# Summing layer 1's first 64 edge columns inside layer 0's last block of a two-layer graph kernel

## The chip, the cores and the metric

The kernel runs on one core of a Trainium2 chip. The metric is the time on the device in microseconds (us) from the start to the end of one launch. The engines have short names here: PE is TensorE's matmul (PEld its weight loads), DVE is VectorE, ACT is ScalarE, POOL is GpSimd, SP is SyncE. Each engine works through its own instructions in the order in which the program issued them, and waits on semaphores where it needs what another engine or a transfer made.

## What is computed

There are 6250 nodes with 256 features each and 100000 edges, sorted by destination, each with a source, a destination and a weight. The reference, cut to what matters:

```python
x = x + gnn0(layernorm(x), src, dst, edge_weight)  # layer 0: node sums over edges, and x @ weight_r
x = x + ffn0(layernorm(x))                         # 8 experts, all used, 256->256->256->256, gated by a softmax
x = x + gnn1(layernorm(x), src, dst, edge_weight)  # layer 1: segment_sum(w * h[src], dst), h = layernorm(x) @ weight
x = x + ffn1(layernorm(x))                         # 32 experts, one per node by argmax, 256->64->256, relu
```

In layer 0 the edges run the other way: row `src` gets the features of `dst`. In layer 1 row `dst` gets those of `src`. Any node may be the source of any edge, so the sum for the first destinations of layer 1 can need the layer-0 result of every node, the last ones too.

## The kernel before, in words

Nodes lie in 49 tiles of 128 (the last has 106). `X` (line 81) keeps all of them in SBUF. `h0` and `h1` (lines 82, 83) are the normalised features of both layers in DRAM, from which edges gather.

**Sort, lines 113 to 538.** The edges come sorted by destination. The first part of the kernel sorts them into tiles of sources for layer 0: `Z` and `ZJ` hold, for each tile of 128 sources, the edges' destinations and weights by group of 4096 edges. It also computes `h0` and the first part of `X`.

**Summing edges.** A column is 128 edges. `weighted` (line 211) gathers their 128 rows of 256 floats with one indirect DMA issued on POOL (line 187), splits the weighted rows into two parts `m` on ACT (line 215) and DVE (line 216); `one_hots` (line 204) makes 0/1 matrices for three columns at once on DVE (line 207); one matmul per column adds it into PSUM `acc` (lines 610 and 777). Layer 0 has 18 columns for each tile, 882 in all. Layer 1 takes the edges as they come, 782 columns (`NREAL`), 8 of which (`CS`) cover on average half a tile; each is matched to a window of half a tile, and neighbouring windows are added (`summed`, lines 752 to 766). `by_weight` (line 191) then turns a tile's sum, multiplies it by the layer's weight and adds it to `X`.

**Dense part.** Layer 0 works in 15 blocks of `1, 1, 2, 3, 4 x 10, 2` tiles (line 287): `begin0` normalises and computes the gates, then for each of 8 experts `hidden0` runs twice (L654, L657) and `outs0` adds the gated product to `X` (L666, L668). `end0` (line 671) normalises a finished block, adds the bias and stores its rows of `h1` (line 680, on SP's queue). Layer 1 works in 16 blocks of `1, 1, 2, 3, 4 x 9, 3, 2, 1` tiles (line 289): `begin1` (line 787) normalises, picks each node's expert and makes the masks, then 16 chunks of two experts each run `hidden1` (L822, L825, L827) and the output matmul (L861); line 868 and the stores after it end a block.

**What sets the order.** The program is written in the order of the PE. `Stream.upto` (line 298) advances the column generator, one column a step, and `aheads` (line 303) plans how many columns are to be issued before each half expert or half chunk, so that the columns of block b+1 are all summed within block b: in the first `parts - rest` places those of the next block, in the last `rest` (4 of 16 in layer 0, 8 of 32 in layer 1) a share of those of the block after. A layer's first block waits for all its columns (lines 687, 837). Gathers run ahead of their use by the buffers of `g`: 12 in layer 0 (line 609), 24 in layer 1 (line 776).

**Between the layers.** After the last `outs0`, line 708 calls `end0` for the last block; its store must land before any gather of layer 1. Then `aggregate_any` (line 711) loads a flag into registers and branches around a loop for badly distributed edges, which isn't run with these inputs. Only then does layer 1 load its weights (lines 716 to 737, 4 MB on ACT's queue) and issue its first gather.

Of the kernel before, what the change touches and what calls it, by code (L numbers as in the profile page):

```python
# [39 lines left out]
LAG = 10  # L40
FAR = -2.0 ** 127
SRC_PAD = 8191
LN_EPS = 1e-5
# [4 lines left out]
def gnn_ffn_kernel(ctx: ExitStack, tc: tile.TileContext, a, out):  # L48

# [35 lines left out]
    def across(name):  # L85

        row = a[name]
        t = const.tile([P, row.shape[0]], F32, name=name + "_b")
        nc.scalar.dma_start(t, bass.AP(tensor=row.tensor, offset=row.offset, ap=[[0, P], [1, row.shape[0]]]))
        return t  # L90
# [15 lines left out]
    good = const.tile([P, 1], F32, name="good")  # L106
    off = const.tile([P, 1], F32, name="off")
    edges_rec, edges_val = a["edges_rec"], a["edges_val"]
# [3 lines left out]
    kept = sorted_ctx.enter_context(tc.tile_pool(name="kept", bufs=1))  # L112
# [63 lines left out]
    bias0 = across("L0_gnn_bias_l")  # L176
    bias0r = across("L0_gnn_bias_r")
# [13 lines left out]
    def by_weight(psum, sums, sT, t, tags):  # L191

        tr = psum.tile([P, 2, P], F32, tag=tags[0], name="tr", bufs=1)
# [4 lines left out]
        ph = psum.tile([P, D], F32, tag=tags[1], name="ph", bufs=tags[2])  # L198
# [5 lines left out]
    def one_hots(pool, dl, j, hots):  # L204

        s = pool.tile([P, SJ, P], F32R, tag="s", name="s", bufs=hots)
        nc.vector.tensor_tensor(s, col[:, None, :].to_broadcast([P, SJ, P]),  # L207
                                dl[:, j:j + SJ, None].to_broadcast([P, SJ, P]), OP.is_equal)
# [10 lines left out]
    def aggregate_any(h, by_dst):  # L219
# [3 lines left out]
        with tc.tile_pool(name="any", bufs=1) as pool, \  # L223
                tc.tile_pool(name="anyp", bufs=1, space=bass.MemoryType.PSUM) as psum:
            with tc.If(flag > 0):
                with tc.For_i(0, ROWS, P) as r:
# [7 lines left out]
                    for t in range(NT):  # L234
# [14 lines left out]
                        for _ in by_weight(psum, sums, sT, t, ("tr", "mm", 2)):  # L249
                            pass  # L250

# [35 lines left out]
    ramp = [1, 1, 2, 3] + [NB] * 10 + [2]  # L287
    blocks0 = [list(range(sum(ramp[:b]), sum(ramp[:b + 1]))) for b in range(len(ramp))]
    ramp = [1, 1, 2, 3] + [NB] * 9 + [3, 2, 1]
# [13 lines left out]
    def aheads(cum, parts, rest):  # L303
# [4 lines left out]
        for b in range(len(cum) - 2):  # L308
# [16 lines left out]
    def check_edges():  # L325
# [26 lines left out]
        nc.vector.tensor_copy(badis[1], bads[1])  # L352
        nc.vector.tensor_scalar(off, bads[1], float(DST_PAD), None, op0=OP.mult)
        nc.vector.tensor_scalar(dl_c, dl_c, off, None, op0=OP.add)
# [182 lines left out]
    nc.vector.tensor_scalar(good, bads[0], 1.0, None, op0=OP.is_lt)  # L537
    sort_ctx.close()
# [4 lines left out]
    with tc.tile_pool(name="layer0", bufs=1) as wp, \  # L543
# [57 lines left out]
        def aggregate0():  # L601
# [13 lines left out]
            while True:  # L615
                yield
# [305 lines left out]
```

## Time and profile before

| what | us |
|---|---|
| median of 3 runs without a profile (2944.88 to 2947.58) | 2945.19 |
| the profiled execution | 3303.56 |
| its span, first to last instruction | 3301.8 |
| sort, until the first gather of layer 0 | 0 to 399.5 |
| layer 0, until its last expert's matmuls | 399.5 to 1946.9 |
| layer 1: first gather at 1956.4, first matmul of an expert's mask at 2046.8 | 1946.9 to 3301.8 |

The profiled execution is 358 us longer than the median without a profile. Its mean granted TensorE clock is 0.926. The engines were busy for these shares of the span: PE 85%, PEld 55%, DVE 60%, ACT 49%, POOL 58%. POOL's busy time is nearly all gathers: 882 in layer 0 (902.8 us) and 782 in layer 1 (773.8 us).

How to read the views: the page cuts the span into 40 slices of 82.5 us, each a digit, the busy share in tenths. The windows view gives the same for any stretch in us, with the number of instructions. The view of waits says which engine and line waited for which, total, times and longest in us. The timeline lists instructions by start and duration, merged where they repeat; what stands in square brackets is how long the engine was idle just before, and what ended it. The chain is the work that ended last, followed back from the end; "another core or an unknown queue" is a wait whose end the profile can't put down to an instruction.

### The profile page before, as it was taken

What the parts mean: (1) busy time and instruction counts of PE and PEld (TensorE: products, weight loads), DVE (VectorE), ACT (ScalarE), POOL (GpSimd) and SP (SyncE); (2) the same over time, 40 slices, a digit from 0 to 9 for tenths busy, and PEclk for the clock granted to TensorE, in tenths of its full rate; (3) what the DMA queues carried; (4) which work ended last, traced back from release to release, by engine and by line L of the source; (5) the groups of instructions that cost most, each with busy time, mean ns of one, the idle gap of its engine ahead of it and who ended that gap; (6) DMA issues with size and microseconds to landing.
All of it is one profiled execution on the core that took longest, in us unless ns stands there. A gap on an engine that the chain in (4) does not pass through costs nothing.

```text
span 3301.8 us, 37412 instructions
## 1 busy us (share of the span) xinstructions
PE 2794.1 (85%) x10471; PEld 1817.4 (55%) x10524; DVE 1993.7 (60%) x4839; ACT 1626.1 (49%) x3842; POOL 1904.3 (58%) x1931
## 2 busy tenths in 40 slices
PE   5888667689999999999999964677898888988899
PEld 3444346555555555555555553555665555656577
DVE  8999856577766765655655433555555555545451
ACT  6778445445555554554554433444444444444442
POOL 4566565676666666566665126666666556656520
PEclk8999877899999999999999986788999999989999
DMA  4000232233323323233332033332333223323210
GB/s 132 20 20 20 81 107 77 80 90 86 90 82 91 88 79 89 85 87 85 88 91 72 26 91 89 89 92 83 92 94 92 86 82 92 93 86 90 86 47 10
DMA packets 123155, 260.73 MB, mean 79 GB/s; under 512 B 32252, under 2 KB 68920, under 8 KB 122936
## 3 DMA queue, kind: packets, MB, share of 16 engines
q0 software_dynamic: 79872, 218.21, 23.2%
q1 hardware_dynamic: 26984, 28.08, 2.5%
q10 hardware_dynamic: 16080, 11.94, 1.3%
q8 instruction: 86, 1.41, 0.2%
q14 instruction: 133, 1.09, 0.1%
HBM read 238.87 MB, written 19.25 MB: 78 GB/s over the span
## 4 chain that ended last, share of the span: by engine, by line
PE 61%; issue 5%; another core or an unknown queue 4%; DVE 3%; ACT 2%; POOL 1%; DMA 0%; ACTq 0%; DVEq 0%; POOLq 0%
PE ph L654 16%; PE py L861 10%; PE ph L822 9%; PE py L666 9%; PE acc L777 6%; PE acc L610 5%; PE ph L200 1%; ACT m L215 1%; DVE m L216 1%; PE ph L825 1%; PE tr L269 1%; PE pl L795 1%; POOL g L187 1%; PE py L644 1%
## 5 line engine op out<-in xcount | busy, mean ns | idle before, releaser
L187 POOL DMA_INDIRECT g<-h,idx x882 | 902.8, 1024 | 547.3 <-DVE m L216 286.6
L187 POOL DMA_INDIRECT g<-h,src_c x782 | 773.8, 990 | 442.3 <-DVE m L216 187.5
L215 ACT ACTIVATE m<-g,of_z 128x256 fp32r<-128x256 f32 x882 | 391.7, 499 | 336.0 <-PE acc L610 135.9
L215 ACT ACTIVATE m<-g,val_c 128x256 fp32r<-128x256 f32 x782 | 371.1, 502 | 374.7 <-PE acc L777 172.0
L657 ACT ACTIVATE hT<-ph,shift,scale 128x512 f32<-128x512 f32 (+3 forms) x480 | 331.0, 697 | 417.1 <-PE ph L654 246.9
L216 DVE SCALAR_TENSOR_TENSOR m<-g,val_c,m 128x256 fp32r<-128x256 f32 x782 | 360.8, 481 | 242.7 <-ACT m L215 133.0
L861 PE MATMUL py<-w,hm 128*128 128x256 f32 x1568 | 415.4, 400 | 35.0 <-issue 17.5
L666 PE MATMUL py<-wo,hT 128*128 128x256 f32 x1568 | 390.3, 390 | 61.1 <-issue 30.6
L216 DVE SCALAR_TENSOR_TENSOR m<-g,of_z,m 128x256 fp32r<-128x256 f32 x882 | 398.0, 477 | 56.6 <-ACT m L215 40.2
L654 PE MATMUL ph<-nT,w 128*128 128x512 f32 (+3 forms) x960 | 385.9, 537 | 44.5 <-ACT hT L657 37.6
L777 PE MATMUL acc<-m,s 128*128 128x512 f32 x782 | 367.9, 534 | 52.6 <-DVE m L216 39.6
L822 PE MATMUL ph<-nT,w 128*128 128x512 f32 (+3 forms) x1024 | 396.8, 509 | 3.5 <-issue 3.1
L610 PE MATMUL acc<-m,s 128*128 128x512 f32 x882 | 356.1, 506 | 46.2 <-DVE scale L567 26.1
L654 PE MATMUL ph<-hT,w 128*128 128x512 f32 (+3 forms) x960 | 375.1, 525 | 23.6 <-issue 17.4
L666 PEld LDWEIGHTS py<-wo,hT 128*128 128x128 f32 x1568 | 292.1, 193 | 141.7 <-issue 46.3
L861 PEld LDWEIGHTS py<-w,hm 128*128 128x128 f32 x1568 | 301.0, 201 | 92.1 <-issue 21.9
L827 ACT ACTIVATE hm<-ph,b 128x512 f32<-128x512 f32 (+3 forms) x256 | 149.1, 584 | 290.8 <-PE ph L825 115.1
L207 DVE TENSOR_TENSOR s<-col,dl 128x384 fp32r<-128x384 f32 x294 | 162.4, 554 | 210.3 <-PE acc L610 142.8
L654 PEld LDWEIGHTS ph<-nT,w 128*128 128x128 f32 x960 | 179.4, 200 | 199.3 <-issue 139.6
L668 DVE SCALAR_TENSOR_TENSOR X<-py,gate,X 128x256 f32<-128x256 f32 x392 | 187.9, 481 | 164.9 <-PE py L666 78.8
L207 DVE TENSOR_TENSOR s<-col,dl_c 128x384 fp32r<-128x384 f32 x261 | 144.2, 553 | 231.6 <-PE acc L777 135.6
L654 PEld LDWEIGHTS ph<-hT,w 128*128 128x128 f32 x960 | 178.7, 196 | 144.9 <-issue 118.7
(206 smaller groups left out, 3267.1 us busy)
## 6 DMA issues: line engine op xcount, KB each, us to landing
g<-h,idx POOLq DMA_INDIRECT x882
g<-h,src_c POOLq DMA_INDIRECT x782
h<-hs SPq DMA_DIRECT2D x26, 256.0 KB
X<-in_x_dram SPq DMA_DIRECT2D x12, 512.0 KB
w<-in_L_ffn_W_dram ACTq DMA_DIRECT2D x3, 2048.0 KB
h<-hs SPq DMA_DIRECT2D x10, 512.0 KB
out_dram<-o SPq DMA_DIRECT2D x9, 512.0 KB
wo<-in_L_ffn_Wo_dram ACTq DMA_DIRECT2D x1, 2048.0 KB
```

The costliest lines, as they stand in the source:

```text
L187: nc.gpsimd.indirect_dma_start(out=g, out_offset=None, in_=h, in_offset=bass.IndirectOffsetOnAxis(ap=idx, axis=0))
L207: nc.vector.tensor_tensor(s, col[:, None, :].to_broadcast([P, SJ, P]), dl[:, j:j + SJ, None].to_broadcast([P, SJ, P]), OP.is_equal)
L215: nc.scalar.activation(m[:, 0, :], g, AF.Copy, scale=w)
L216: nc.vector.scalar_tensor_tensor(m[:, 1, :], g, w, m[:, 0, :], op0=OP.mult, op1=OP.subtract)
L610: nc.tensor.matmul(acc, s[:, j % SJ, :], m, start=(j == 0), stop=(j == EW - 1))
L654: nc.tensor.matmul(ph[:, :nw], (w1, w2)[layer][:, e, k, m * P:(m + 1) * P], src[:, k, :nw], start=(k == 0), stop=(k == 1))
L657: nc.scalar.activation(hT[:, m, :nw], ph[:, :nw], AF.Relu, bias=shift[:, layer, c:c + 1], scale=scale[:, layer, c:c + 1])
L666: nc.tensor.matmul(py, hT[:, k, j * P:(j + 1) * P], wo[:, e, k, :], start=(k == 0), stop=(k == 1))
L668: nc.vector.scalar_tensor_tensor(X[:, t, :], py, gate[:, j, e:e + 1], X[:, t, :], op0=OP.mult, op1=OP.add)
L777: nc.tensor.matmul(acc, s[:, j % SJ, :], m, start=(i == 0 or j == 0), stop=done)
L822: nc.tensor.matmul(ph[:, :nw], w1f[:, k, c * P:(c + 1) * P], nT[:, k, :nw], start=(k == 0), stop=False)
L861: nc.tensor.matmul(py[:, j, :], now[:, cols], w2[:, c, :], start=False, stop=(c == NC1 - 1), skip_group_check=True)
```

## The change

The change does the following.

- `columns1` takes the place of `aggregate1`. It sums a range of columns. The first range, columns 0 to 63 (`NE = EARLY * GC`), is appended to layer 0's own column stream and planned into layer 0's last block, from its third half expert on. It gathers from `h1[:LIM]`, the rows of all blocks but the last; an edge whose source lies in the last block gets weight 0 and a harmless index. Its sums stay in `first_sums` (5 tiles). The second range, columns 64 to 781, runs in layer 1.
- `missing` builds, from the sorted `Z` and `ZJ` of layer 0, for each of the last block's 3 tiles a matrix (128 sources x 576 destinations) of the weights of those edges of the first 64 columns that were left out, in four matmuls per pair of pieces; it does so in the last block's experts 5, 6 and 7, in the space of `wo`'s first experts. `add_missing` multiplies them by the last block's normalised rows and adds the product to `first_sums`.
- Layer 0's blocks become `1, 1, 2, 3, 4 x 9, 3, 3`, layer 1's `3, 4 x 11, 2`. The store of the block before the last moves from expert 1 to expert 0 of the last block.
- The sums of layer 1's first block (3 tiles) come from `first_sums`, so `by_weight` of these tiles runs right after `end0` of the last block, before any further gather is used.
- Layer 1's weights take the memory of layer 0's `w1` and `w2`. They are loaded in halves from SP's queue at experts 4 and 7 of the last block. The small ones are loaded three blocks before the end. `sel` is made on DVE behind the first `begin1`.
- `aggregate_any` for layer 1 moves to the very end, with a rerun of all of layer 1's dense part (`again`) that the flag skips with these inputs. PSUM and SBUF pools are shared across the layers, and with `reuse_waits="tile"` a tile that reuses memory waits for that memory's users alone.
- `edges0` works on two tiles at a time instead of four.

```diff
-    ramp = [1, 1, 2, 3] + [NB] * 10 + [2]
+    ramp = [1, 1, 2, 3] + [NB] * 9 + [3, 3]
     blocks0 = [list(range(sum(ramp[:b]), sum(ramp[:b + 1]))) for b in range(len(ramp))]
-    ramp = [1, 1, 2, 3] + [NB] * 9 + [3, 2, 1]
+    ramp = [3] + [NB] * 11 + [2]
...
+    def columns1(pool, psum, js, h, idx, w, bufs):
+        hots, ahead, parts, few = bufs
+        first = js.start == 0
+        ends = []
+        def summed(q, acc):
+            yield
+            if first and (q % 2 or q == 2 * NB):
+                s = first_sums[:, q // 2, :]
+            else:
+                s = pool.tile([P, D], F32, tag="sums", name="sums", bufs=few)
+            nc.scalar.activation(s, acc[:, 0, :], AF.Copy)
+            nc.vector.tensor_add(s, s, acc[:, 1, :])
...
+        for j in range(js.start, js.stop + (0 if first else LAG)):
+            if j < js.stop:
...
+                if (j - js.start) % SJ == 0:
+                    s = one_hots(pool, dl_c, j, hots)
+                m = weighted(pool, h, idx[:, j:j + 1], w[:, j:j + 1], ahead, parts)
+                nc.tensor.matmul(acc, s[:, (j - js.start) % SJ, :], m, start=opens, stop=done)
...
@@ aggregate0
+            for _ in columns1(wp, psum, range(NE), h1[:LIM, :], idx_e, w_e, (3, 12, 6, 2)):
+                yield
@@ end0
-                nc.vector.tensor_add(X[:, t, :], X[:, t, :], bias1)
             nc.sync.dma_start(h1[tiles[0] * P:(tiles[0] + n) * P, :].rearrange("(t p) d -> p t d", p=P),
                               hs[:, :n, :])
+            for t in tiles:
+                nc.vector.tensor_add(X[:, t, :], X[:, t, :], bias1)
+            return hs
+        def load1(k, half):
+            if k == 0:
+                x = a["L1_ffn_W1"][:, half * P:(half + 1) * P, :].rearrange("e p h -> p e h")
+                nc.sync.dma_start(w1f[:, half, :].rearrange("p (e h) -> p e h", h=H1), x)
+            else:
+                cs = slice(half * NC1 // 2, (half + 1) * NC1 // 2)
+                x = a["L1_ffn_W2"].rearrange("e h d -> (e h) d").rearrange("(c p) d -> p c d", p=P)
+                nc.sync.dma_start(w2f[:, cs, :], x[:, cs, :])
+        def missing():
+            nc.gpsimd.iota(near, pattern=[[1, NEAR]], base=0, channel_multiplier=0,
+                           allow_small_or_imprecise_dtypes=True)
...
+            for i in range(n_late):
+                pms = [psum.tile([P, 4 * P], F32, tag="mm", name="pm", bufs=3),
+                       psum.tile([P, wide], F32, tag="tr", name="pm_tr", bufs=1)]
+                for c in range(EARLY):
+                    to = wp.tile([P, NEAR], F32R, tag="there", name="to_m", bufs=1)
+                    nc.vector.tensor_scalar(to, near, dst[:, i, c:c + 1], None, op0=OP.is_equal)
...
+                    for u in range(2):
...
+                        nc.tensor.matmul(pms[0], of[:, u, :], to[:, :4 * P], **flags)
+                        nc.tensor.matmul(pms[1], of[:, u, :], to[:, 4 * P:], **flags)
+                nc.scalar.activation(mats[i][:, :4 * P], pms[0], AF.Copy)
+                nc.scalar.activation(mats[i][:, 4 * P:], pms[1], AF.Copy)
+                yield
+        def add_missing(hs, fs):
+            corr = psum.tile([P, 2, D], F32, tag="mm", name="corr", bufs=3)
+            for u, f in enumerate(fs):
+                rows = min(P, NEAR - f * P)
+                for i in range(n_late):
+                    nc.tensor.matmul(corr[:rows, u, :], mats[i][:, f * P:f * P + rows], hs[:, i, :],
+                                     start=(i == 0), stop=(i == n_late - 1))
+                nc.vector.tensor_add(first_sums[:rows, f, :], first_sums[:rows, f, :], corr[:rows, u, :])
...
+        head = 2
+        plans[-1] = [cum[-1] + NE * max(0, u + 1 - head) / (2 * NX0 - 1 - head) for u in range(2 * NX0 - 1)]
+        plans[-1] += [cum[-1] + NE + 1]
...
             for e in range(NX0):
-                if e == 1 and b > 0:
+                if e == (0 if final else 1) and b > 0:
                     end0(blocks0[b - 1])
+                if b == nblk - 3 and e == 3:
+                    small1()
+                    early_columns()
+                if final and e == 5:
+                    fill = missing()
+                if final and e >= 5:
+                    next(fill)
                 sums.upto(plans[b][2 * e])
                 second = hidden0(1, block, e, first)
...
+                if final and e in (NX0 // 2, NX0 - 1):
+                    load1(0, e // (NX0 // 2 + 1))
+                    load1(1, e // (NX0 // 2 + 1))
                 sums.upto(plans[b][2 * e + 1])
                 outs0(block, e, second)
...
-        end0(blocks0[-1])
+        hs = end0(late)
+        add_missing(hs, (0, 1))
+        add_missing(hs, (2,))
+        firsts = []
+        for t in blocks1[0]:
+            sT = wp.tile([P, 2, P], F32, tag="hT0", name="sT", bufs=2)
+            firsts.append(by_weight(psum, first_sums[:, t, :], sT, t, ("agg", 2) if t else ("tr", 1)))
+            next(firsts[-1])
+        for part in firsts:
+            next(part)
+        add_missing(hs, (3, 4))
-    aggregate_any(h1, by_dst=True)
...
+            sums = Stream(columns1(flow, psum, range(NE, NREAL), h1, src_c, val_c, (5, EW + 6, 12, 4)))
+            cum = [0] + [min(CS * (2 * tiles[-1] + 2) + CS // 2, NREAL) + LAG - NE for tiles in blocks1[1:]]
+            plans = aheads(cum, 2 * NC1, [4] + [8] * (len(blocks1) - 1))
+            block = begin1(flow, blocks1[0])
...
+                    if c == NC1 - (3 if b == 0 else 5) and not last:
+                        after = begin1(flow, blocks1[b + 1])
+                end1(flow, tiles, py)
...
+            aggregate_any(psum, h1, True, again)
```

## The prediction

> **What bounds the kernel now.** I first read the page's slices, to see where no engine is full.
>
> ```profile
> span 3301.8 us, 37412 instructions
> PE   5888667689999999999999964677898888988899
> POOL 4566565676666666566665126666666556656520
> PEclk8999877899999999999999986788999999989999
> ```
>
> There are two holes. POOL falls to 1 and 2 around slice 23, in the middle of the span: no gathers in the last part of layer 0. PE falls to 4 and 6 just after that: layer 1 has begun and its matmuls have nothing to work on. The windows view cuts the passage at what happens in it; columns are the stretch, its length, busy us (instructions) of the five engines, granted clock, DMA share and GB/s.
>
> ```profile
> 1850.00:1947.00 97.00, 96.89 (x382) 69.86 (x380) 30.91 (x82) 39.31 (x66) 0.00 (x0) 1.00 0.02 6
> 1947.00:1957.00 10.00, 0.00 (x0) 0.10 (x1) 5.21 (x17) 0.36 (x2) 2.79 (x3) 0.75 0.16 45
> 1957.00:1985.00 28.00, 11.39 (x18) 5.16 (x18) 14.34 (x36) 10.21 (x23) 21.60 (x22) 0.50 0.91 246
> 1985.00:2047.00 62.00, 19.33 (x51) 11.94 (x51) 16.70 (x48) 17.37 (x40) 41.14 (x42) 0.56 0.30 88
> 2047.00:2322.00 275.00, 207.49 (x859) 158.88 (x860) 144.14 (x369) 118.94 (x288) 180.07 (x181) 0.84 0.30 89
> 2322.00:2822.00 500.00, 432.38 (x1622) 291.86 (x1649) 263.57 (x646) 219.72 (x494) 314.08 (x320) 0.94 0.30 89
> 3197.00:3302.00 105.00, 99.25 (x494) 78.52 (x493) 21.00 (x60) 31.68 (x74) 0.00 (x0) 0.99 0.04 13
> ```
>
> Layer 0 ends with 97 us of full PE and an idle POOL. From 1947 to 2047 PE does 31 us of work, at half clock, while POOL gathers. From 2047 to 2322, the one-, two- and three-tile blocks of layer 1, PE is at 75%, POOL at 181 gathers in 275 us. Only then come the steady blocks of 4 tiles, and the last 105 us are PE alone. The timeline shows the seam.
>
> ```profile
> 1949.72 0.36 SPq L680 DMA_DIRECT2D h<-hs  x1
> 1954.05 2.04 POOL L740 IOTA sel<- 128x2048 bf16 x1 [112.07 <-DMA h<-hs]
> 1956.38 1.28 POOL L187 DMA_INDIRECT g<-h,src_c  x1 [0.17 <-issue]
> 1963.45 0.95 POOL L187 DMA_INDIRECT g<-h,src_c  x1 [0.30 <-issue]
> 1969.24 2.50 PE L777 MATMUL acc<-m,s 128*128 128x512 f32 x5 [22.36 <-DVE m L216]
> 2321.72 0.61 PE L855 MATMUL py<-nought 128*128 128x512 bf16 x2
> ```
>
> POOL waited 112 us for the last store of `h1`. An unhindered gather takes 0.95 + 0.30 = 1.25 us. The last row opens the block of tiles 7 to 10; the next ones open 100.3 us apart on average (five blocks to 2823.2). So 374.8 us lie between layer 0's last matmul (1946.9) and tile 7. Last, the waits, and the chain's row for one of them:
>
> ```profile
> ACT m L215 <- remote: 28.1, 12, 17.9
> POOL g L187 <- DVE m L216: 23.1, 28, 3.6
> 2025.58 17.88 another core or an unknown queue x2
> ```
>
> In those 375 us POOL is hardly held back (23.1 us); it is the pace: tile 7 needs 180 columns plus a lag of 10 and 16 ahead, 206 x 1.25 = 258 us after 1956.4, that is 2214 at best. But 50.5 us of the chain there are waits on an unknown queue, one of them 17.9 us, and in the five steady blocks 63.3, 12.7 each. The profiled execution is 3303.6 us against a median of 2945.2; I take these waits as what is likeliest to be missing from a plain run, and sum both with and without them.
>
> **The change part by part.**
>
> *Final block of layer 0.* Two tiles take 5.18 us an expert (L666 groups at 1910.40 and 1915.58), so three take 7.77, 62.2 in all. It now has 64 columns as well. On PE a column costs 0.21 us (two weight loads of L777 take 0.41 at full clock), 13.7 us; `missing` adds 24 short matmuls, about 4. On ACT 64 x 0.50 = 32 beside 21 for L657; on DVE 64 x (0.48 + 0.18) = 42, plus 12 for the gated adds (24 x 0.48), 10 for `missing` (six of about 0.65, by L207's 0.55 for 384 columns, twelve of 0.25, sixteen of 0.2) and 6 for `end0`. All fit below 100 us; POOL is what counts: `end0`, with its table load, took 8.5 us from its first statistics (1905.1) to the issue and a store 3.8 to land, so about 11 us with three tiles; then 64 x 1.25 = 80, then 6 for landing, scaling, matmul and the last `outs0`. The iota of `missing` stands in POOL's queue and waits for `outs0` of expert 4, which waits for the columns before it: everything gathered after it loses the lead, about 7. Sum 104: layer 0 ends 42 us later than it would (its total dense work is the same with 3, 3 as with 4, 2). Bounds: 35 with no hold by the iota, 59 at the 275/181 = 1.52 us a gather of the small blocks.
>
> *The 4 MB of weights.* They leave the seam and join these gathers. The trace: from 1957 to 1985 both ran together, 0.91 of the DMA engines busy, and POOL still issued 22 gathers in 28 us, 1.27 each; but the first gather, issued at 1956.4, was used at 1968.2. Against the move speaks the Trainium skill, DMA: Bandwidth & Descriptors, "Issuing engines are not separate DMA queues": the queue that issues changes only the time to issue, all transfers share the same 16 engines. By the rule the loads cost the gathers the engine time they took, 28 x 0.91 less 22 gathers at the 0.30 x 1.5 us of the steady rows, about 16 us of a 104 us block with 28 us of gathers: under half full. By the row, 12 us of latency, which the 12 buffers (15 us of gathers) cover. I take 3, for the second half beside the last store of `h1` on SP's queue; 0 to 12.
>
> *The seam.* `end0` took 2.8 us for two tiles here, so 4 for three, and the store 4.5: gathers resume 9 us after layer 0's end, without the branch and the weight loads ahead of them. PE meanwhile: corrections 3 to 5, `by_weight` of three tiles 5, `begin1` of three about 15 (nine turns of PE, ACT and DVE at 0.3 to 0.5 each way, six DVE steps of 0.29): experts start 30 us after layer 0's end instead of 100. Here the clock matters. The rows grant 0.50 to 0.56 in the seam. The Trainium skill, TensorE: Matmul & The Clock Gate, Part 1, has the clock halve after an idle window of 3.4 us; so by rule and row the seam's 12 us of small matmuls stay cold, included above. The rule also threatens the final block, now paced by POOL with PE 80% busy; the nearest row (2047 to 2322, 75% busy) shows 0.84, which makes 80 us of PE work 95, still below 104: nothing.
>
> *Blocks 0 and 1.* Block 0's experts need 45 us for 3 tiles and 13 for columns; block 1 needs 62 more columns: 9 + 62 x 1.25 + 4 = 91 us after layer 0's end, 107 at 1.52; I take 98. Block 1 is a steady one, 100. Tile 7 starts 42 + 98 + 100 = 240 us after the old end of layer 0, not 374.8: 135 earlier.
>
> *After tile 7.* The same 42 tiles remain with as many columns ahead (202 against 206), but the old blocks 3, 2, 1 ran nearly free of gathers (100 us), and so did the 73 of the block before. The new order is eight full blocks (802), one with 56 columns (93), one with 24 (67), two tiles (31), and 5 to the end: 999, plus 3 for the flag's branch that now stands behind everything (0 to 10; here it was hidden by the store, and the first one took 2 from 391.6). Before: 980. So 22 come back.
>
> *Hidden edits.* `edges0` in pairs: 10.0 us of DVE a block for 9.2 (rows of 2.03 and 1.09), under a DVE at 60%; uncovered it would be 8 in all. `small1` makes DVE wait for three small loads once, 0 to 5, PE's two `py` buffers hide most. The store one expert earlier and the bias after it cost nothing. Tiles that reuse layer 0's memory may hold the first gathers; no row shows that, 0 to 10 by the seam's 10 us between matmul and gather, and I take 5.
>
> **Sum.** In the profile's own time: -135 + 22 + 3 + 5 = -105, 3304 to about 3199. Without the unknown waits: the passage before is 375 - 50 = 324; after, 42 + 91 + 88 = 221 (blocks at 100.3 - 12.7 = 87.6); afterwards 14 come back; -103 + 14 + 3 + 5 = -81. Since the passage also had 43 us of unexplained issue time, some of which a plain run may not have either, I take -70: 2945 - 70 = 2875.
>
> **The rivals.**
>
> *Smaller gain, 0.20.* The small blocks are slow not for gathers but for each block's chain through `begin1`: the old three-tile block took 100 us (2219 to 2319). If the new block 0 takes as long from its start at 30, tile 7 is at 42 + 130 + 100 = 272: 103 earlier instead of 135, or -81 + 32 = -49, and with the same allowance -45: 2900. For it: PE waits there for ACT and DVE in many small sums. Against: POOL never rested for long.
>
> *The whole, 0.12.* A plain run has the same stalls as the profile: -105 to -115, 2835.
>
> *Slower, 0.07.* The final block starves. Early gathers, weight halves and stores meet on the DMA engines, layer 0's pool has only 12 buffers, and the plan lets every half expert wait for its columns in PE's order. The price is 64 times the extra spacing. Break-even is where this eats the 70 us: 1.25 + 70/64 = 2.35 us a gather; at 3 us the time is 2945 - 70 + 112 = 2987. For it: 12 us to the first use when weights were loading. Against: 1.27 us spacing in that very stretch.
>
> *It doesn't do what it says, 0.03.* The early gathers are held (by memory or the store) until the dense work is nearly over; then they cost after it what they cost at the start of layer 1 before, and the time is 2945.
>
> The likeliest, 0.58, spans 2850 to 2898. The range reaches from the larger gain to the far end of the smaller one with its bounds: 2832 to 2925. A measurement of this kernel can tell about 0.2%, 6 us, from no change: faster 0.90, same 0.03, slower 0.07.
>
> **What would show it.** In the profile after: gathers of columns 0 to 63 inside the last block, spaced near 1.25 us; that block about 100 us long; resumed gathers within 10 us of the last expert's matmul; experts of layer 1 within 35; tile 7's block about 195 us after it; fewer than 80 us from the last gather to the end, where it was 129 (from 3172). I am wrong if the early gathers are spaced over 2 us, or if tile 7 comes later than 270.

## The result, and the profile after

The changed kernel takes 2912.77 us (median of 4 runs, 2906.32 to 2920.75) against 2946.39 for the kernel before: a ratio of 0.9887, 95% interval 0.9859 to 0.9915. It is faster, by 34 us, where 70 was forecast. The two profiled executions below are 41 apart, since the changed kernel's was the fastest of its four (2906.32). The kernel before takes 2946 us on three of the chips used below and 3256 to 3260 on two others, so every experiment stands beside the kernel before on its own chip; the profile that the forecast was read from (3303.6 us, granted clock 0.926) has stalls, where the plain runs beside it took 2945 us, and may come from such a slower chip (clocks of 0.926 to 0.937 for the kernel before there), which is not shown. A second profile of the kernel before, at 2947.16 us, is compared from here on; it has no wait on an unknown queue.

The page of the changed kernel, its first rows and slices (72.6 us each):

```profile
span 2904.5 us, 36970 instructions
PE   5888848889999999999999998779999999999998
POOL 4666667777767666776675527577777777777720
PEclk9999969999999999999999998989999999999999
```

And of the kernel before, in the second profile (73.6 us each):

```profile
span 2945.4 us, 37465 instructions
PE   5888848888999999999999995788999999999999
POOL 3566667777767766666666404777777777777730
```

The hole of POOL (4 and 0) has become 5, 5 and 2, and the 5 of PE behind it a 7. The slices of layer 1 behind the passage are alike: PE at 9, POOL at 7, in both. So the steady part of layer 1 runs no faster; what differs lies in the passage and, as an experiment below shows, a little in layer 0. The windows view gives the sizes; columns as in the prediction. After:

```profile
1727.00:1841.00 114.00, 91.80 (x309) 60.78 (x308) 65.34 (x161) 51.48 (x108) 66.67 (x66) 0.91 0.39 118
1841.00:1955.00 114.00, 89.76 (x351) 62.89 (x351) 71.05 (x176) 55.74 (x125) 87.24 (x85) 0.89 0.33 97
1955.00:2051.00 96.00, 92.44 (x351) 62.24 (x355) 62.58 (x154) 51.77 (x113) 73.71 (x73) 0.96 0.36 105
2200.00:2700.00 500.00, 490.27 (x1938) 338.25 (x1969) 323.85 (x773) 270.50 (x590) 383.95 (x382) 1.00 0.36 107
2784.00:2904.50 120.50, 112.22 (x472) 79.84 (x475) 17.90 (x53) 28.18 (x56) 1.10 (x2) 0.98 0.05 15
```

Before:

```profile
1797.00:1900.00 103.00, 56.84 (x223) 39.28 (x224) 54.82 (x145) 44.21 (x108) 78.67 (x75) 0.66 0.48 135
1900.00:2000.00 100.00, 78.89 (x363) 62.24 (x361) 62.30 (x154) 53.06 (x129) 77.00 (x76) 0.88 0.35 102
2000.00:2092.00 92.00, 78.64 (x321) 56.13 (x321) 59.30 (x145) 49.21 (x110) 70.71 (x70) 0.94 0.35 104
2200.00:2700.00 500.00, 490.86 (x1971) 338.15 (x1970) 325.99 (x779) 269.23 (x592) 383.62 (x383) 1.00 0.37 107
2826.00:2945.40 119.40, 113.91 (x556) 88.87 (x555) 28.99 (x81) 37.77 (x87) 1.35 (x2) 0.99 0.05 15
```

From some 5 us behind layer 0's end to about tile 7, PE is idle 81 us in the three windows before and 28 in the two after (1841 to 2051); but the stretch ahead of them, layer 0's last block, now has 22 idle us of 114. The steady 500 us are the same to 0.6 us of PE work and one gather. The timeline rows of the gathers at the ends, after:

```profile
1730.62 0.94 POOL L201 DMA_INDIRECT g<-h,idx_e  x1 [48.90 <-DVE X L762]
...
1815.39 0.95 POOL L201 DMA_INDIRECT g<-h,idx_e  x1 [0.30 <-issue]
...
1831.35 3.33 PE L760 MATMUL py<-wo,hT 128*128 128x256 f32 x12
...
1840.95 0.94 POOL L201 DMA_INDIRECT g<-h,src_c  x1 [24.62 <-PE corr L878]
...
2784.46 0.95 POOL L201 DMA_INDIRECT g<-h,src_c  x1 [0.30 <-DVE rstd L332]
```

and before, first and last gather of layer 1:

```profile
1801.55 1.29 POOL L187 DMA_INDIRECT g<-h,src_c  x1 [0.17 <-issue]
...
2826.71 0.94 POOL L187 DMA_INDIRECT g<-h,src_c  x1 [0.30 <-issue]
```

These rows close the account. From the first gather of layer 1 to the last, POOL pauses at most 0.31 us between two gathers, in both kernels, with one pause of 1.48 us in the changed one: nothing holds it up, so the gathers' own spacing is the pace. Before, 781 steps from the first to the last gather take 1025.2 us, 1.313 each; after, 717 steps take 943.5 us, 1.316 each. Sixty-four gathers fewer are 84.0 us; gathers resume 39.4 us later (1840.95 against 1801.55); the slightly wider spacing costs 2.4; the tail behind the last gather is 120.0 us against 118.7. 84.0 - 39.4 - 2.4 - 1.3 = 40.9, the difference of the two spans.

### The profile page after: what moved, and what is told of

The parts are those of the page before. It is cut to its first block, busy times and chain, and to the rows that moved or that the text cites. A ratio compares the mean times of both kernels' runs of the same rounds, so it can differ in the third digit from the quotient of the medians.

```text
span 2904.5 us, 36970 instructions
## 1 busy us (share of the span) xinstructions
PE 2685.0 (92%) x10276; PEld 1750.0 (60%) x10336; DVE 2017.1 (69%) x4917; ACT 1626.5 (56%) x3790; POOL 1921.2 (66%) x1932
## 4 chain that ended last, share of the span: by engine, by line
PE 60%; DMA 10%; issue 6%; DVE 5%; ACT 3%; POOL 2%; another core or an unknown queue 0%; ACTq 0%; POOLq 0%; SPq 0%; DVEq 0%
PE ph L748 19%; PE py L760 10%; PE py L999 8%; PE ph L983 8%; PE acc L701 6%; DMA g<-h,src_c 5%; PE acc L277 4%; DMA g<-h,idx 3%; POOL g L201 2%; DVE m L231 2%; ACT m L230 2%; DMA g<-h,idx_e 1%; PE ph L214 1%; PE tr L340 1%; PE pl L720 1%
## 5 line engine op out<-in xcount | busy, mean ns | idle before, releaser
L201 POOL DMA_INDIRECT g<-h,src_c x718 | 724.9, 1010 | 244.2 <-issue 110.8
L230 ACT ACTIVATE m<-g,w 128x256 fp32r<-128x256 f32 x882 | 393.9, 500 | 254.5 <-PE acc L701 130.7
L231 DVE SCALAR_TENSOR_TENSOR m<-g,w,m 128x256 fp32r<-128x256 f32 x882 | 397.3, 476 | 44.4 <-ACT m L230 43.5
L748 PE MATMUL ph<-nT,w 128*128 128x512 f32 (+3 forms) x960 | 376.1, 527 | 25.0 <-ACT hT L751 24.9
L999 PE MATMUL py<-w,hm 128*128 128x256 f32 x1568 | 385.2, 384 | 2.0 <-ACT hm L988 1.9
L983 PE MATMUL ph<-nT,w 128*128 128x512 f32 (+2 forms) x832 | 377.2, 574 | 0.0
L701 PE MATMUL acc<-m,s 128*128 128x512 f32 x882 | 339.7, 488 | 37.1 <-DVE scale L657 24.7
L277 PE MATMUL acc<-m,s 128*128 128x512 f32 x782 | 335.4, 502 | 5.7 <-DVE m L231 5.4
L748 PEld LDWEIGHTS ph<-nT,w 128*128 128x128 f32 x960 | 176.9, 197 | 175.1 <-issue 119.6
L988 ACT ACTIVATE hm<-ph,b 128x512 f32<-128x512 f32 (+2 forms) x208 | 136.8, 659 | 194.7 <-PE ph L986 141.9
L701 PEld LDWEIGHTS acc<-m,s 128*128 128x128 f32 x882 | 169.2, 195 | 108.9 <-issue 50.1
L983 PEld LDWEIGHTS ph<-nT,w 128*128 128x128 f32 x832 | 158.0, 192 | 102.2 <-issue 81.8
```

What stands on the lines that cost most here:

```text
L201: nc.gpsimd.indirect_dma_start(out=g, out_offset=None, in_=h, in_offset=bass.IndirectOffsetOnAxis(ap=idx, axis=0))
L230: nc.scalar.activation(m[:, 0, :], g, AF.Copy, scale=w)
L231: nc.vector.scalar_tensor_tensor(m[:, 1, :], g, w, m[:, 0, :], op0=OP.mult, op1=OP.subtract)
L277: nc.tensor.matmul(acc, s[:, (j - js.start) % SJ, :], m, start=opens, stop=done)
L701: nc.tensor.matmul(acc, s[:, j % SJ, :], m, start=(j == 0), stop=(j == EW - 1))
L748: nc.tensor.matmul(ph[:, :nw], (w1, w2)[layer][:, e, k, m * P:(m + 1) * P], src[:, k, :nw], start=(k == 0), stop=(k == 1))
```

## The experiments

Three theories were tested. **G**: layer 1 moves at the pace of its gathers, from the first to the last. **S**: each early gather stalls PE in its program order, whatever other work is there. **P**: PE bounds layer 1 wherever its work is at hand, and only its idle time can be won. (In the first expectation, S stands for the chain of each block, the forecast's *smaller gain*.)

| run | us | before on that chip | ratio, 95% interval |
|---|---|---|---|
| before_again | 2947.16 | 2946.15 | a single run |
| early_no_gather | 2881.60 | 2946.15 | 0.9787 (0.9773 to 0.9800) |
| no_fix | 2901.82 | 2946.15 | 0.9853 (0.9838 to 0.9869) |
| late4 | 2911.97 | 2946.15 | 0.9886 (0.9871 to 0.9901) |
| late24 | 3259.51 | 3256.36 | 0.9997 (0.9977 to 1.0017) |
| after_no_gather1 | 2996.18 | 3256.36 | 0.9182 (0.9148 to 0.9217) |
| before_no_gather1 | 2977.31 | 3256.36 | 0.9130 (0.9097 to 0.9162) |
| after_half_pe | 3219.62 | 3256.36 | 0.9883 (0.9837 to 0.9928) |
| after_again | 3227.90 | 3260.40 | 0.9895 (0.9867 to 0.9923) |
| late24_again | 3256.00 | 3260.40 | 0.9991 (0.9976 to 1.0005) |
| before_ramp | 3264.31 | 3260.40 | 1.0010 (0.9994 to 1.0026) |
| half_pe_again | 3212.32 | 3260.40 | 0.9859 (0.9829 to 0.9889) |
| first33 | 2905.38 | 2945.45 | 0.9860 (0.9845 to 0.9875) |
| late4b | 2899.21 | 2945.45 | 0.9843 (0.9830 to 0.9857) |
| both | 2894.62 | 2945.45 | 0.9829 (0.9816 to 0.9843) |
| plain_loads | 2858.07 | 2945.45 | 0.9703 (0.9689 to 0.9718) |
| before_pairs | 2939.24 | 2946.49 | 0.9975 (0.9967 to 0.9984) |
| half_pe_3 | 2907.57 | 2946.49 | 0.9858 (0.9843 to 0.9874) |

"Below the changed kernel" is said against its 2912.77 us, where the kernel before takes 2946; it was not run again on those chips, and its four runs lie 14 us apart. So a difference of some 10 us or less is read together with the trace.

**A clean profile of before** (before_again, no edit).

> The kernel before, unchanged, for a second profile: the first one has stalls on an unknown queue that the profile of the changed kernel has not. Theory G (gathers set the pace of layer 1): the changed kernel's profile shows one gather per 1.31 us from its first to its last gather of layer 1. Then here too: layer 0 ends near 1795, 782 gathers of 1.31 us take 1024, the last gather is near 2828, 117 us of dense work follow, 2945. Tile 7 opens about 300 us after layer 0's end. Theory S (each block's chain through the router and the normalisation sets the pace, as in the rival with the smaller gain): gathers spaced unevenly, 1.4 or more in the small blocks, and tile 7 at 324 or later.

2947.16 us. It gave the rows of before shown above. Its full blocks of layer 1 end 83 to 86 us apart; in the profile of the forecast it was 100.3.

**What the last block of layer 0 pays** (early_no_gather, no_fix).

```diff
-            for _ in columns1(wp, psum, range(NE), h1[:LIM, :], idx_e, w_e, (3, 12, 6, 2)):
+            for _ in columns1(wp, psum, range(NE), None, idx_e, w_e, (3, 12, 6, 2)):   # no gather: a constant row
```

> The changed kernel; its first 64 columns scale rows of a constant in SBUF instead of gathered rows (their 64 gathers are left out, all else stays). Theory G: the last block of layer 0 is paced by these gathers, 112 us for 82 of work, so it falls to about 82 and the time by 30, to 2883. If the columns themselves (scaling, matmul, plan) or the correction pace the block, it stays within 10 us of 2913.

2881.60, 31 us below the changed kernel. The stretch that held 22 idle us of PE:

```profile
1727.00:1812.00 85.00, 81.41 (x307) 57.15 (x306) 61.18 (x157) 48.22 (x104) 0.97 (x2) 0.98 0.19 59
```

Without the gathers PE is busy 81 of 85 us and the last store of `h1` is issued at 1808.1 instead of 1837.7. So 30 us of the last block are waits for gathered rows, and they reach the end undiminished: 29.6 us there, 31 in the total.

```diff
-                    fill = missing()
+                    fill = iter(range(4))
...
-        add_missing(hs, (0, 1))
-        add_missing(hs, (2,))
-        add_missing(hs, (3, 4))
```

> The changed kernel without the correction: the matrices of the last block's edges and their products are left out, so edges from the last block are missing in the first 64 columns. By the profile, the last matrix stands between the last early column (1821) and the last expert's second layer (1828), and 4 us of corrections stand in the seam: 8 to 12 us less, 2903. If all of it is hidden: 2913.

2901.82, 11 us below: the price of the correction, as expected within 2 us. The trace agrees: from the last early gather to the end of layer 0 it is 11 us (1816.5 to 1827.7) instead of 19.

**A longer last block** (late4, late24, late24_again, late4b). The layer-0 blocks `1, 1, 2, 3, 4 x 9, 3, 3` become the following; a last block of four tiles also gets a fourth correction matrix.

```diff
+    ramp = [1, 1, 2, 1] + [NB] * 11          # late4
+    ramp = [1, 1, 2, 3] + [NB] * 9 + [2, 4]  # late24, late24_again
+    ramp = [1, 1, 3] + [NB] * 11             # late4b
```

> The changed kernel with a last block of 4 tiles in layer 0 (1, 1, 2, 1, then 11 of 4) and a fourth correction matrix, built in the space of the index row. Theory G: 20.7 us more of dense work stand beside the same 64 gathers, so the last block is no longer stretched by 36 but by about 18: 2913 - 18 + 3 for the fourth matrix = 2898. Theory S: the stretch is not what costs; one more matrix and one more tile in the seam's chain, 2916.

> The changed kernel with the last two blocks of layer 0 cut 2, 4 instead of 3, 3 (start-up blocks untouched; a fourth correction matrix with its eight matmuls). The last block of layer 0 opens one tile, about 20.7 us of matmuls, earlier, and so do the 64 early gathers. In the changed kernel's last stretch (1727 to 1841 us) TensorE was idle 22 us. Theory G (a steady layer 1 moves at one gather per 1.31 us) and theory P (TensorE is the bound wherever its work is there, and only its idle time in the passage can be won) both say: the 22 us of idle TensorE are filled with the fourth tile's work, less about 4 us for the extra correction: 2905 - 17 = about 2888 to 2893. Theory S (each early gather stalls TensorE in its program order whatever work is around): 2908 to 2914, as changed.

> The changed kernel with the last two blocks of layer 0 cut 2, 4, beside the changed kernel on the same chip. Theory P (TensorE bounds, only its idle time can be won): the fourth tile's 20.7 us of matmuls fill most of the 22 us that TensorE was idle in the last stretch of layer 0, less about 4 for the fourth correction matrix: 13 to 18 us below the changed kernel, so 2888 to 2899 where the kernel before takes 2946. Theory S (an early gather stalls TensorE in its program order whatever work is around): within 5 us of the changed kernel.

> The changed kernel with layer 0 in blocks of 1, 1, 3 and eleven of 4: the last block has 4 tiles, and the block before it is a full one, so its own columns aren't squeezed into a block of 2 tiles. If idle TensorE in the last stretch (22 us) is what early gathers cost, and the start-up with one small block fewer costs at most 8: 5 to 12 us below the changed kernel (ratio to before 0.984 to 0.987). If the start-up loses what the end wins, as with blocks of 1, 1, 2, 1 and eleven of 4: within 4 us of it.

late4 equalled the changed kernel (2911.97), which spoke for S. Its trace says otherwise: from 1720 to 1840 PE is busy 109 us instead of 98, as wanted, but from 440 to 800, where the first blocks of layer 0 differ (1, 1, 2, 1 instead of 1, 1, 2, 3), it is idle 9 us more. late24 was a mistake of mine, and lost all of the gain twice: its two-tile block has to take in all 72 columns of the four-tile block behind it, so the last layer-0 gather came at 1834.6 instead of 1812.9 (the changed kernel on the same chip). late4b has neither fault (38.5 idle us from 440 to 800, 38.9 in the changed kernel): 2899.21, 14 us below the changed kernel. Its last block:

```profile
1714.00:1830.00 116.00, 104.94 (x349) 64.07 (x348) 71.46 (x177) 56.07 (x111) 65.13 (x65) 0.99 0.39 118
```

11 idle us of PE instead of 22: with more matmuls beside them, the same 64 gathers cost less. S falls.

**Gathers or PE** (after_no_gather1, before_no_gather1, plain_loads; after_half_pe, half_pe_again, half_pe_3).

```diff
-            sums = Stream(columns1(flow, psum, range(NE, NREAL), h1, ...))    # after_no_gather1
+            sums = Stream(columns1(flow, psum, range(NE, NREAL), None, ...))
-                    m = weighted(wp, h1, src_c[:, j:j + 1], ...)              # before_no_gather1
+                    m = weighted(wp, None, src_c[:, j:j + 1], ...)
-        g = gather(pool, h, idx, ahead)                                       # plain_loads
+        if ahead == EW + 6 and h is h1:     # layer 1's second range
+            g = pool.tile([P, D], F32, tag="g", name="g", bufs=ahead)
+            nc.sync.dma_start(g, h[:P, :])
+        else:
+            g = gather(pool, h, idx, ahead)
```

> The changed kernel without the gathers of layer 1's second range: its 718 columns scale a constant row instead of gathered rows, so the output's sums are not the reference's; everything else is kept. Steady blocks of 4 tiles now take 84 us, TensorE busy 82.6 of them and GpSimd never held more than 0.3 us. Theory G (gathers at 1.31 us are the pace): blocks fall to the matmuls' own time, at most 78 us, and the total by 6 us for each of 9 blocks plus some 20 us of the passage: 2825 to 2840. Theory P (TensorE is the pace, gathers only just keep up): blocks stay at 82 to 84 us and only the idle TensorE between layer 0's end and tile 7 (28 us from 1841 to 2050) shrinks: 2880 to 2895.

> The kernel before without layer 1's gathers: its 782 columns scale a constant row, so the output's sums are not the reference's. TensorE was idle about 81 us between 1797 and 2100. Theory G: blocks fall below 78 us, total by 60 us and more beyond the passage: 2800 to 2840. Theory P: blocks stay at 82 to 84 us; of the 81 idle us perhaps 50 were waits for gathered rows, so 2885 to 2900; and then it lies within 15 us of the changed kernel without its gathers.

> The changed kernel with each of the 718 gathers of layer 1's second range replaced by an ordinary load of the same size from SyncE's queue, always the first 128 rows of h1 (the sums are not the reference's). The bytes moved stay, the indirect DMA is gone. Where the kernel before takes 2946: blocks 82.2 to 83 us instead of 84, total 2880 to 2895. Where it takes 3256: if the stalls that stretch blocks from 82 to 99 us there come with the indirect DMAs, blocks fall to 82 to 84 and the total to about 3000 to 3030; if they come with the bytes on the DMA engines, blocks stay above 95 and the total above 3190.

Without gathers a block of 4 tiles takes 82.2 us in all three (82.1 to 82.5), on a chip with stalls and on one without. The totals of the first two missed because layer 0, which still gathers, kept its stalls there; the blocks are as P has them. On that chip, without layer 1's gathers, the changed kernel is 19 us slower than the kernel before: the early columns bring nothing of their own, they only shorten the line of gathers. plain_loads came out 55 us below the changed kernel, more than expected (its loads always fetch the same 128 rows, so what the scattered rows cost is not told apart from what the indirect transfer costs):

```profile
1841.00:1955.00 114.00, 109.71 (x469) 78.86 (x467) 87.43 (x224) 65.95 (x157) 0.00 (x0) 0.97 0.51 151
...
2200.00:2700.00 500.00, 499.44 (x2007) 344.59 (x2006) 327.39 (x792) 269.27 (x601) 0.00 (x0) 1.00 0.37 109
```

PE is full in the steady stretch, and in block 0 it is idle 4 us instead of 24. Block 0's outputs are stored 89 us after the last store of `h1` instead of 118, and 89 in after_no_gather1 too. Now the other side:

```diff
-                nc.tensor.matmul(acc, s[:, (j - js.start) % SJ, :], m, start=opens, stop=done)
+                nc.tensor.matmul(acc[:, 0, :], s[:, (j - js.start) % SJ, :], m[:, 0, :], start=opens, stop=done)
-            nc.vector.tensor_add(s, s, acc[:, 1, :])
+            nc.vector.tensor_add(s, s, acc[:, 0, :])
```

> The changed kernel with layer 1's gathers kept but half of TensorE's work on them left out: each column's matmul takes only the high half of the weighted rows (256 columns, not 512), so the low halves are missing from the sums. GpSimd's own floor is 1.25 us a gather, 80 us for 64. Theory P: steady blocks fall from 84 to 80 or 81 us, where the gathers hold them, spacing 1.25 to 1.27, and the total by 30 to 45: 2860 to 2875. Theory G: blocks stay near 84, total within 10 us of the changed kernel: 2895 to 2905.

> The changed kernel with layer 1's gathers kept and half of TensorE's work on each column left out (only the high half of the weighted rows is summed). Where the kernel before takes 2946: theory P: steady blocks fall from 84 to 80 or 81 us, to the gathers' own floor of 1.25 us each, the total to 2865 to 2880. Theory G (gathers at 1.31 us are the pace): blocks stay at 84, 2898 to 2908.

> The changed kernel with layer 1's gathers kept and half of TensorE's work on each column left out (the low halves are not summed). Where the kernel before takes 2946: theory P (TensorE's own 82.2 us bound a steady block, gathers come next at 1.25 us each, 80): blocks 80 to 81 us, total 2865 to 2885. Theory G (gathers at 1.31 are the pace): blocks 83 to 84, total 2898 to 2908. Where it takes 3256, as in two runs before: near 3215, and nothing is told apart.

Two runs fell on chips with stalls (blocks of 98 us) and tell nothing here. The third:

```profile
2200.00:2700.00 500.00, 461.17 (x1943) 323.19 (x1975) 325.39 (x780) 275.17 (x592) 383.48 (x383) 0.97 0.37 107
```

PE has 29 us less to do in 500, and as many gathers get done: 383. Eight full blocks end 83.8 us apart on average, 84.2 in the changed kernel. The total, 2907.57, is 5 us below the changed kernel, which is within its spread; G had 2898 to 2908, P 2865 to 2885. So both theories hold a half. With gathers a block takes 64 x 1.31 = 84 us and gathers set it, as G has it; PE alone needs 82.2, as P has it, and is 2% behind. My floor of 1.25 us a gather was too low as a mean: POOL pauses 0.30 us and still averages 1.31, since 28% of the changed kernel's gathers in layer 1 take more than 1.00 us instead of 0.95 (mean 1.01). In these blocks a step that relieves one of the two alone gains at most 2%.

**Which part of the change** (after_again, before_ramp, before_pairs). after_again is the changed kernel; the others are the kernel before with one part of the change (before_ramp also takes over the store of outputs that the new blocks need):

```diff
-    ramp = [1, 1, 2, 3] + [NB] * 10 + [2]           # before_ramp, layer 0
+    ramp = [1, 1, 2, 3] + [NB] * 9 + [3, 3]
-    ramp = [1, 1, 2, 3] + [NB] * 9 + [3, 2, 1]      # before_ramp, layer 1
+    ramp = [3] + [NB] * 11 + [2]
...
-            at = wp.tile([P, NB, EW, NG + 1], BF, tag="at", name="at", bufs=1)   # before_pairs: edges0
...
+            for i in range(0, n, 2):
...
+                at = wp.tile([P, 2, EW, NG + 1], BF, tag="at", name="at", bufs=1)
...
```

> The changed kernel as it is, beside the next three on one chip. Where the kernel before takes about 2946 us: 2906 to 2920, ratio 0.987 to 0.991. Where it takes about 3256 us (a steady block of layer 1 there took 99 us with its gathers and 82.2 without): theory P wins only idle TensorE in the passage, ratio 0.98 to 1.0.

> The kernel before with only the new block sizes (3, 3 at the end of layer 0; 3, eleven of 4, 2 in layer 1) and the changed kernel's store of outputs; no early gathers and no correction. Theory P: the first experts of layer 1 now wait for 62 columns instead of about 20, so TensorE is idle some 95 us in the passage instead of 81; the one- and two-tile blocks' short matmuls cost TensorE perhaps 15 us more than full blocks do, and that is saved: together 2935 to 2960. If the new sizes by themselves made the gain, it would be near 2910.

> The kernel before with only the edge lists of layer 0 built in pairs of tiles, as in the changed kernel. Of the 42 us by which TensorE is idle less after the change, 11 lie before layer 0's last block, most of them near 600 to 700 us, where in the kernel before VectorE stood 10 us in the middle of an edge list (676.6 us). If the pairs are the cause: 5 to 11 us below the kernel before, ratio 0.996 to 0.9985. If that wait is chance or comes with another part: within 3 us of it, ratio 0.999 to 1.001.

On a chip with stalls the change gives 0.9895, about what it gives without. The new block sizes alone give nothing on that chip (1.0010). The paired edge lists alone give 7 us, with an interval clear of 1: a gain that the forecast had at zero. The kernel before has this row, with PE waiting 10.3 us behind it:

```profile
676.63 0.20 DVE L591 TENSOR_SCALAR idx<-bothi 128x72 int32<-128x72 int32 x1 [10.04 <-DMA g<-h,idx]
```

VectorE stands, in its own order, before the write of an index list whose buffer gathers are still reading; the `outs0` additions that PE needs are queued behind it. In before_pairs the list is written 8 us later (675.1, where VectorE began to stand at 666.6), and the wait is gone; PE is idle 11 us of the stretch from 600 to 700 instead of 19.

**Fewer columns ahead of block 1** (first33, both).

```diff
-    ramp = [3] + [NB] * 11 + [2]
+    ramp = [3, 3] + [NB] * 10 + [3]
```

> The changed kernel with layer 1 in blocks of 3, 3, ten of 4, 3 instead of 3, eleven of 4, 2: block 1 needs 16 columns fewer before it opens. In the changed kernel block 0 ended 121 us after layer 0, though it takes about 92 without gathers. Theory W (block 0's last steps wait for block 1's 62 columns at 1.4 us each): block 0's outputs come 20 to 24 us earlier, but block 1 with 3 tiles has only 66 us of matmuls for 64 columns and gives most of it back; total 5 to 12 us below the changed kernel (ratio to before 0.985 to 0.987). Theory C (the chain of small operations into block 1 sets it, not the columns): block 0's outputs less than 8 us earlier, total within 4 us of the changed kernel.

> Both of the above: layer 0 in 1, 1, 3 and eleven of 4, layer 1 in 3, 3, ten of 4, 3. If both act at different places their gains add: 10 to 22 us below the changed kernel (ratio to before 0.981 to 0.985).

first33: block 0's outputs come 96.3 us after the last `h1` store instead of 118.2, 21.9 sooner for 16 columns, 1.37 each; block 1 takes 91 us for three tiles and gives most of it back; 2905.38 in all, as the columns' theory W has it. The total alone would not tell W from C; the 21.9 us of block 0 do. Both edits together take 2894.62, 18 us below the changed kernel's median and 51 below the kernel before: the fastest version found that leaves nothing out.

## Why the prediction came out too large

**The last block.** Forecast 104 us instead of 62, so layer 0 ends 42 later; it ends 42.3 later (1834.7 against 1792.4), out of two errors that cancel. The block takes 112 us: the gathers 85 instead of 80 (1.34 each), 8 instead of 11 ahead of the first, no hold by the iota where 7 was put, and 19 instead of 6 from the last gather's issue to the end. Of these 19, the third correction matrix takes about 8 (11 are left in no_fix), where the forecast had `missing` hidden under the gathers; and the last gather took 5.5 us to land (other gathers 2.8) beside the second half of the weights. The block starts 7.7 us sooner than 62 us before the old end, and before_pairs gained 7. The loads cost about what was put on them (3, from 0 to 12), as far as the trace shows: besides that landing, the gathers beside the first half (1758.9 to 1785.6) came 1.33 us apart, against 1.35 in the block as a whole, so the 16 us that the forecast worked out by the rule did not show. No run leaves the loads out.

**The seam.** Forecast 9 us to the first resumed gather and 30 to the experts; measured 6.3 and 20.6. The forecast kept the seam's matmuls at the halved clock. The granted clock is 0.93 from 1834.7 to 1855.3, with PE busy 14 of these 20.6 us; it falls to 0.56 only from 1855 to 1860, behind a stretch in which PE was busy 2 us of 5. In the second profile of before it is 0.55 from 1792.4 to 1860, with PE busy 23 of 68 us.

**Blocks 0 and 1: the step that failed.** Forecast without the unknown waits: block 0 over 91 us after layer 0's end, block 1 in 88, tile 7 at 179 after that end. Measured: 121, 96 and 217. The 62 gathers come 1.36 us apart instead of 1.25, 7 us more. And the step that failed is the 4 us put behind the last of them: it is issued at 1923.8, and block 0's outputs are stored at 1955.9, 32 us later. The forecast left out the chain that stands there in PE's order (`by_weight` of block 1's last tile, block 1's normalisation and its transposes), and that ACT, which makes the copies of this chain, takes its work in order. In the stretch from 1831 to 1953 ACT waited:

```profile
ACT m L230 <- DMA g<-h,src_c: 35.2, 47, 4.4
```

and the `sT` and `nT` copies of block 1's chain were queued behind scalings that each wait for a gather of a later column; PE waited up to 5.9 us for one of them. PE has turned the last tile's sum by 1930.0, but its copy `sT` comes at 1937.59; from there the rest of the chain takes 18 us:

```profile
PE ph L214 <- ACT sT L210: 8.3, 3, 5.9
...
1929.56 0.44 PE L209 MATMUL tr<-ident,sums 128*128 128x128 f32 x2
...
1937.59 0.36 ACT L210 ACTIVATE sT<-tr 128x256 f32<-128x256 f32 x1
1938.01 2.07 PE L214 MATMUL ph<-wg,sT 128*128 128x256 f32 x4 [5.86 <-ACT sT L210]
...
1955.88 0.38 SPq L1010 DMA_DIRECT2D out_dram<-o  x1
```

That the order on ACT makes this delay is read from the trace; no run moves the copies to another engine. That gathers make block 0 long is shown by the runs: without them it takes 89 us store to store, with them 118, and 16 columns fewer (first33) win 21.9 of these 29.

On the other side the passage before was read at 324; it is 304 (the outputs of the block ahead of tile 7 are stored at 2096.7, layer 0 ended at 1792.4). So 145 us were forecast to vanish between layer 0's end and tile 7, and 87 did.

**The two yardsticks.** The passage before was taken from a stalled profile, the passage after was built from floors. The forecast had the right rule in hand, POOL is the pace, with 206 gathers before tile 7 opens, and did not apply it to both sides. At 1.31 us: before 9 + 206 x 1.31 = 279, after 6 + 142 x 1.31 = 192. Both are 25 below what was measured: tile 7 opens 21 us behind the 206th gather before (2075.3) and 23 behind the 142nd after (2029.0), a part that the rule leaves out. As it is nearly alike on both sides, the difference, 87, comes out. Less 42 is 45, and 4 us come back later: 41.

**After tile 7.** Forecast 14 + 3 + 5 us back; 4 came (848.7 against 852.8 us from there to the end). The tail of 120 us behind the last gather, forecast under 80, was 119 before as well: the old blocks 3, 2, 1 were no better off than a block of 4 and one of 2. The 11 us of allowance stand for nothing. In sum: 103 - 45 = 58 too much in the passage, 18 too much taken back, 11 too much allowed; 58 - 18 - 11 = 29, from 70 to 41.

**The rivals.** *Smaller gain* came nearest: tile 7 at 42 + 217 = 259 where it had 272. But its cause, the chain into block 1 for itself and not the gathers, is the smaller part: that chain is there without gathers too, and then block 0 takes 89 us. *Slower* had the right place: waits of the last block cost 30 us, but at 1.34 us a gather, far from its 2.35. The other two did not come about.

## What to carry to other kernels

If a profiled execution is 12% slower than the plain runs, profile again before sizing anything: here its stalls widened just the stretch that the change was to shorten. Where one engine issues a fixed number of steps without a break, count steps: the gain is the steps taken out at the spacing of the trace, less the delay of the first one left in, here 64 x 1.31 - 39 = 45, of which 41 were left after a slightly wider spacing and a longer tail; measure before and after with the same rule. And when the next bound is 2% behind, as PE was in the steady blocks, no faster gather brings more than that there.

## What was not expected of the hardware

On two chips the kernel before took 3256 and 3260 us. On the second of them (after_again), PE waits in layer 1 of the changed kernel, from 1980 to 2900 us, up to 15.9 us for other engines and up to 17.0 us for nothing that the profile shows ("issue"):

```profile
PE tr L340 <- DVE xn L346: 42.0, 7, 9.4
PE py L999 <- ACT hm L988: 35.1, 11, 15.9
PE acc L277 <- issue: 23.4, 6, 17.0
```

and a full block takes 99 us. On the first, with the gathers of layer 1 taken out (after_no_gather1), PE is full:

```profile
2161.00:2736.70 575.70, 575.06 (x2311) 396.01 (x2310) 377.56 (x914) 311.21 (x693) 0.00 (x0) 1.00 0.02 7
```

So in that stretch the stalls were gone with the gathers. The Trainium skill, Runtime: NRT & Kernel Launch, "Instruction fetch mechanics", says that each engine streams its instructions through a DMA queue of its own, mostly hidden; instructions held up behind gathers could look like this. The trace speaks against it for the wait of 17.0 us, which ends at 2030.63: from 2000 to 2030.6 all 1062 recorded transfers belong to gathers, none to an instruction queue; and ACT stood 17.0 us too, until 2029.34. plain_loads, which was to tell the indirect transfers from the bytes, ran on a chip without stalls, so the cause stays open.
